# A two-layer decoder: one product buffer of the value stage takes the place of the first key weights

## The chip, the cores and the metric

The kernel runs on one core of a Trainium2 chip. The metric is the device time of one execution in microseconds, the median of several runs; less is better. An execution on the core has five instruction queues that run beside each other and wait for each other by semaphores: PE (matrix products), DVE (vector work), ACT (activations, here often copies out of the accumulator memory PSUM), POOL (a second, slower vector engine) and SP (which here only issues DMAs). Each queue works strictly in its own order.

## What is computed

Two transformer layers over a batch of 4 sequences of 256 tokens, 512 wide, in float32, with a layer norm after each of the four blocks:

```python
x = _layernorm(x + _L0_attn_ref(x, ...))   # attention with low-rank queries, keys and values, 32 heads
x = _layernorm(x + _L0_ffn_ref(x, ...))    # gated feed-forward, integer weights with scales
x = _layernorm(x + _L1_attn_ref(x, ...))   # causal attention, 32 heads
x = _layernorm(x + _L1_ffn_ref(x, ...))    # linear layer plus eight low-rank experts
```

The change touches the second attention only. Its projections are

```python
q = jnp.einsum('bsd,de->bse', hidden_states, wq).reshape(B, S, H, DQ)
kv = jnp.einsum('bsd,de->bse', hidden_states, wkv)
k = kv[..., :H * DN].reshape(B, S, H, DN)
v = kv[..., H * DN:H * (DN + DV)].reshape(B, S, H, DV)
```

where `H` is 32 and `DN` and `DV` are 128. The scores, the causal mask, the softmax, the product with `v` and the output projection follow.

## The kernel before

**Products with fewer multiplications.** Every large product is computed by a scheme of seven block products instead of eight, applied twice, one within the other (7 x 7 products in place of 8 x 8). Each of the seven "outer" products `i` (0 to 6) is itself made by seven "inner" ones. The price is additions: combinations of the input blocks, of the weight blocks (`combinations`, L133, four subtractions or additions at L136 to L139) and of the results.

**The value stage.** It lies between the first feed-forward block and the second attention (about 648 to 832 us of the profile). It makes the values of all 32 heads in four groups `g` of two times four heads (`NV`, `stages_v`). A group is seven units `p`, one for each outer product `i = OUTER[p // 2][p % 2]`, in the order 2, 0, 1, 4, 3, 6, 5. The list `vorder` (L669) puts 28 units in a row: the first two of group 3, the first two of group 2, then the rest of groups 3, 2, 1 and 0.

In a unit, `seven` (L787) issues seven inner products on PE (L969 in `multiply`), each 128 x 512 out, as four matmul records. They go to three PSUM banks; two units in turn use the banks `b0, b1, b2` and `s, t, o`. ACT (L800) and DVE (L803) empty the banks, with the additions of the inner scheme, into a buffer for the outer product `i`. At the end of the unit, `end` adds this buffer to the results by `add` (L952): four additions of 128 x 512, three on POOL and one on DVE, all at L956. `store` (L958, DMA at L962) writes finished values of groups 1 to 3 to DRAM, from where the attention reads them back. Group 0 stays in SBUF.

**The buffers of the outer products.** `block()` hands them out, four in turn: the two halves of `x` (x[0:4] and x[4:8], free here because `x` has been saved to DRAM at L746), then the slots s8 and s9, then s10 and s11. A slot holds 128 x 1024 numbers. The slots s0 to s7 hold results of odd groups. In the attention the twelve slots hold queries and keys.

**What else runs in the stage.** `input_blocks2` (L774), called once in the second unit, makes the combinations of the inputs: some on DVE (L772 and L531 to L534), and three sets (`blocks2(i, nc.gpsimd)`) on POOL. The combined value and query weights were prepared in the first attention and lie in DRAM (`vw`, `qd`); `Stored.get` loads them, three units ahead, by two DMAs on SP into `qb` and `qc` (L504; the query weights by L502), with three buffers each.

**The first key weights.** Key weights are not prepared before. `Weights.load` (L831, DMA at L839) loads 1 MB of one group of four heads into the tile `w`, `combine` makes the outer combinations on POOL (into `c`), and `get` the inner ones (`inner_left`, into `cc`, and partly in place in `w`). For group 0 these three are the first entries of the list `first`: `load`, `combine`, the `get` of the first key unit. The `get` of the first three query units are the entries 3 to 5. The function `begin`, which runs ahead of every value unit, calls them: entries 0, 1 and 2 ahead of the units 21, 22 and 23 of 28, and entries 3, 4 and 5 ahead of the units 25, 26 and 27.

**What sets the order.** The order in which this code issues the work is not the order on the queues: a scheduler orders each engine's instructions when the program is built, by its own estimate of when they can start. The place of a call in the code is a priority, not a position.

**Behind the value stage.** The queries and keys of group 0 follow (L874 in `stages_qk`): first four query units, then four key units. The first of each writes straight into slots; the others write into `parts`, which lie in `x`: the second unit in x[4:8], the third in x[0:4], the fourth in x[4:8] again. `add` at L895 sums them up, half on DVE and half on POOL for group 0. All these products use the banks b0, b1 and b2. The attention itself begins at about 876 us.

Of the kernel before, what the change touches and what calls it, by code (L numbers as in the profile page):

```python
# [9 lines left out]
F32 = mybir.dt.float32  # L10
# [6 lines left out]
P = 128  # L17
# [3 lines left out]
DC = D // P  # L21
NH = 32
GH = 4
NG = NH // GH
DN, DR, DV = 128, 64, 128
# [13 lines left out]
def tile_decoder2(ctx: ExitStack, tc: tile.TileContext, a: dict, out: bass.AP):  # L39
# [497 lines left out]
    with tc.tile_pool(name="f0", bufs=1) as f0:  # L537
# [131 lines left out]
        vorder = [(3, 0), (3, 1), (2, 0), (2, 1)]  # L669
        vorder += [(g, p) for g in (3, 2, 1, 0) for p in range(7) if (g, p) not in vorder]  # L670
        with tc.tile_pool(name="f0d", bufs=2) as f0d:
# [62 lines left out]
            for tt in range(NT // 2):  # L734
# [7 lines left out]
                for m in range(2):  # L742
                    t = 2 * tt + m
# [18 lines left out]
    with banks("ps1", b0=1, b1=1, b2=1, s=2, t=2, o=1), \  # L762
# [11 lines left out]
        def input_blocks2():  # L774

            for t in (NT - 2, NT - 1):
                turned(t, nc.scalar.copy)
            xcomb(3, xblock(1, 1), xblock(0, 1))
            xcomb(4, xblock(0, 1), xblock(0, 0))
            xcomb(1, xblock(1, 1), right[4])  # L780
            blocks2(1)
            blocks2(4)
            xcomb(5, xblock(1, 0), right[1])
            for i in (3, 6, 5):
                blocks2(i, nc.gpsimd)

        def seven(multiply, shape, dst, scale=1.0, tags=("b0", "b1", "b2"), hold="p1", bufs=2):  # L787

            st, o = {}, {}
            b0, b1, b2 = tags  # L790

            def product(i, tag, first):

                if first:
                    st[tag] = bank(tag, (P, *shape))
                multiply(i, st[tag], first)
                return st[tag]

            def copy(key, acc):
                nc.scalar.activation(o[key], acc, AF.Copy, scale=scale)  # L800

            def plus(key, acc, other):
                nc.vector.scalar_tensor_tensor(o[key], acc, scale, o[other], ALU.mult, ALU.add)  # L803

            def first():
                o[None] = l1.tile([P, *shape], F32, tag=hold, name="p1", bufs=bufs)
                o.update({(n, m): dst(n, m) for n in range(2) for m in range(2)})
                copy(None, product(0, b0, True))

            return [  # L810
                first,
                lambda: plus((0, 1), product(1, b1, True), None),
                lambda: plus((1, 1), product(4, b2, True), None),
                lambda: copy((0, 0), product(2, b0, False)),
                lambda: plus((1, 1), product(3, b1, False), (1, 1)),
                lambda: plus((0, 1), product(6, b2, False), (0, 1)),
                lambda: plus((1, 0), product(5, b1, False), None),
            ]
# [46 lines left out]
        def stages_qk(pr, g, store, scale):  # L865
# [3 lines left out]
            def units_of(p):  # L869
# [46 lines left out]

                us = seven(multiply, (len(pair), Q), dst, scale, tags_next())
                us[0] = lambda u=us[0]: (begin(), u())
                us[-1] = lambda u=us[-1]: (u(), end())
                return [(u, len(pair)) for u in us]  # L920
# [3 lines left out]
        def stages_v(g):  # L924

            pr, heads, st = pv[g], (2 * g, 2 * g + 1), {}

            def block(i=None):

                if i is None:  # L930
                    i = turnx[0] = (turnx[0] + 1) % 4
                    if i < 2:
                        return [x[:, 4 * i + 2 * k:4 * i + 2 * k + 2, :] for k in range(2)]
                    i += 2
                return [
                    l1.tile([P, 2, GH * DV], F32, tag=f"s{2 * i + k}", name="vb", bufs=1) for k in range(2)
                ]

            def result(n, m):

                if (n, m) not in st:
                    if g % 2:
                        st[n, m] = block(2 * n + m)
                    else:
                        h = heads[n]
                        if h not in v:
                            v[h] = l1.tile([P, NT, GH * DV], F32, tag="v", name=f"v{h}")
                        for mm in range(2):
                            st[n, mm] = [v[h][:, 4 * mm + 2 * k:4 * mm + 2 * k + 2, :] for k in range(2)]
                return st[n, m]  # L950

            def add(out, l, r):  # L952
                for k in range(2):
                    for t in range(2):
                        eng = nc.vector if k and t else nc.gpsimd
                        eng.tensor_tensor(out[k][:, t], l[k][:, t], r[k][:, t], ALU.add)  # L956

            def store(n, m):  # L958
                if g:
                    for k in range(2):  # L960
                        t0 = 4 * m + 2 * k
                        nc.sync.dma_start(out=vd[heads[n]][:, t0:t0 + 2, :], in_=st[n, m][k])  # L962

            def stage(p, tags):
                i = OUTER[p // 2][p % 2]

                def multiply(k, acc, first):
                    for t in range(2):
                        nc.tensor.matmul(  # L969
                            acc[:, t, :].rearrange("p (h c) -> p h c", h=2),  # L970
                            inner[i][k][:, t * P:(t + 1) * P], pr.inner[i][k],
                            start=first and t == 0, stop=True, skip_group_check=True,
                        )

                def dst(n, m):
                    if n == m == 0:
                        st[i] = result(0, 0) if i == 2 else result(0, 1) if i == 0 else block()
                    return st[i][m][:, :, n * 2 * DV:(n + 1) * 2 * DV]

                def end():  # L980
                    u = st.get(0)
                    if i == 0:
                        add(st[2], st[2], u)
                        store(0, 0)
                    elif i == 1:
                        add(u, u, st[1])
                    elif i == 4:
                        add(result(1, 1), u, st[4])
                    elif i == 3:
                        add(result(1, 0), u, st[3])  # L990
                    elif i == 6:
                        add(u, st[1, 1], st[6])
                        store(0, 1)
                        add(st[1, 1], st[1, 1], st[3])
                        store(1, 1)
                    elif i == 5:
                        add(st[1, 0], st[1, 0], st[5])
                        store(1, 0)

                us = seven(multiply, (2, 2 * DV), dst, tags=tags)  # L1000
                us[-1] = lambda u=us[-1]: (u(), end())
                return us

            return stage
# [139 lines left out]
        for g in range(NG):  # L1144
# [10 lines left out]
            else:  # L1155
                first = [wk.load, wk.combine, *(st["ahead"] for st in (sk[0], *sq[:3]))]
# [28 lines left out]
        for n, us in enumerate(vunits):  # L1185
            def begin(n=n, u=us[0]):
                if n + 3 < len(vorder):
                    later = vorder[n + 3]
                    pv[later[0]].get(later[1])
                else:  # L1190
                    first[n + 6 - len(vorder)]()
                if len(vorder) - 7 <= n < len(vorder) - 4:
                    first[n + 7 - len(vorder)]()
                u()
                if n == 1:
                    input_blocks2()

            us[0] = begin
# [3 lines left out]
        def units_of(stages):  # L1202

            units = []
            for st in stages:
                def begin(st=st):
                    for key in ("load", "att", "next"):
                        if key in st:
                            st[key]()

                (u, w), rest = st["units"][0], st["units"][1:]
                units += [((lambda begin=begin, u=u: (begin(), u())), w), *rest]
            return units
# [197 lines left out]
```

## Time and profile before

| | |
|---|---|
| median of 3 runs | 1683.13 us (1682.35 to 1692.36) |
| the profiled execution: time | 1681.63 us |
| the profiled execution: span of the core's work | 1679.6 us |
| mean granted PE clock | 0.997 of full speed |
| PE busy | 1644.5 us, 98% of the span |
| DVE busy | 1064.9 us, 63% |
| ACT busy | 700.8 us, 42% |
| POOL busy | 1104.5 us, 66% |
| chain that ended last | PE 88%, DVE 7%, POOL 2%, DMA 1%, ACT 1% |

All places below are microseconds from the start of the span. A line of a timeline gives the start, the duration, the engine, the source line, the operation, the output and inputs by the program's names, how many instructions were merged, and in brackets how long the engine stood idle before and what ended that. "SPq" is SP's queue, which issues DMAs. A duration of merged instructions covers all of them.

In the stages around the change PE's matmuls follow each other at one record in 0.216 us when nothing stops them. What counts in this profile is where PE does not keep that pace.

### The profile page before, as it was taken

Reading aid. Unit: us, or ns where it says so; the run is one execution under the profiler, and the core shown is the slowest. Engines: PE = TensorE matmul, PEld = TensorE weight load, DVE = VectorE, ACT = ScalarE, POOL = GpSimd, SP = SyncE. Lnnn points to the kernel's source line nnn. Section 1 sums busy time; section 2 is a strip of 40 time slices with the busy share of each in tenths; the row PEclk is TensorE's granted clock in tenths of the full one; section 3 lists DMA queues with packets and bytes.
Section 4 is the critical chain, followed back from the end, with each engine's and each line's share of the span. In section 5 each row is a group of like instructions: output and inputs, shape, how many; then the busy total and the mean of one; then the engine's idle time right before and its main releaser. Section 6 shows DMA issues by size and latency. Waiting matters only on the chain.

```text
span 1679.6 us, 24076 instructions
## 1 busy us (share of the span) xinstructions
PE 1644.5 (98%) x7954; PEld 1294.9 (77%) x7954; DVE 1064.9 (63%) x2345; ACT 700.8 (42%) x2070; POOL 1104.5 (66%) x1330
## 2 busy tenths in 40 slices
PE   8999999999999998999999999999999999999998
PEld 5566666666488887888878888888888878888854
DVE  3577777777745536677777666666666775433454
ACT  1566666667422202111125555555555553200043
POOL 1988888881437445786667767677676777689530
PEclk9999999999999999999999999999999999999999
DMA  9465555451312002687524334253342344443000
GB/s 345 152 211 215 217 199 205 175 194 50 108 43 77 13 26 73 200 262 248 187 76 128 115 98 144 71 178 118 95 140 73 122 176 161 155 151 125 26 18 33
DMA packets 96251, 226.88 MB, mean 135 GB/s; under 512 B 10272, under 2 KB 53792, under 8 KB 90112
## 3 DMA queue, kind: packets, MB, share of 16 engines
q1 hardware_dynamic: 94464, 224.54, 38.9%
q8 instruction: 63, 1.03, 0.3%
q10 hardware_dynamic: 1664, 0.81, 0.2%
q14 instruction: 60, 0.49, 0.1%
HBM read 140.38 MB, written 84.93 MB: 134 GB/s over the span
## 4 chain that ended last, share of the span: by engine, by line
PE 88%; DVE 7%; POOL 2%; DMA 1%; ACT 1%; issue 1%; DVEq 0%; SPq 0%; POOLq 0%; ACTq 0%
PE ps_b L874 19%; PE ps_s L63 13%; PE ps_b L1059 11%; PE ps_b L969 5%; PE ps_o L1135 4%; PE ps_o L396 3%; PE ps_s L612 3%; PE ps_t L379 3%; PE ps_p L294 3%; PE ps_t L1126 2%; PE ps_o L63 2%; PE ps_t L969 2%; PE ps_o L612 2%; PE ps_p L612 2%; PE ps_b L63 2%; PE ps_p L302 2%
## 5 line engine op out<-in xcount | busy, mean ns | idle before, releaser
L1108 ACT ACTIVATE pr<-ps_s,nmx 128x128 f32<-128x128 f32 (+1 forms) x256 | 105.0, 416 | 105.0 <-DVE nmx L1104 101.9
L355 ACT ACTIVATE pr<-ps_s,ebias 128x256 f32<-128x256 f32 x256 | 117.7, 472 | 48.5 <-DVE ebias L350 46.9
L1068 DVE TENSOR_TENSOR x<-ps_b,x 128x512 f32<-128x512 f32 x96 | 66.2, 690 | 105.0 <-PE ps_b L1059 97.5
L63 PE MATMUL ps_s<-kT,qh 128*128 128x256 f32 x512 | 129.1, 393 | 1.1 <-ACT pr L355 1.1
L1120 ACT ACTIVATE pr<-pr,rc 128x128 f32<-128x128 f32 (+1 forms) x256 | 103.8, 448 | 56.6 <-DVE rc L1118 55.0
L1100 DVE TENSOR_TENSOR ps_s<-ps_s,mask 128x256 f32<-128x256 f32 x128 | 55.2, 431 | 106.5 <-PE ps_s L63 106.5
L63 PEld LDWEIGHTS ps_s<-kT,qh 128*128 128x128 f32 x512 | 91.5, 189 | 37.6 <-issue 20.2
L803 DVE SCALAR_TENSOR_TENSOR x<-ps_b,p 128x512 f32<-128x512 f32 (+1 forms) x159 | 96.3, 607 | 22.9 <-PE ps_b L874 13.3
L344 DVE TENSOR_REDUCE nmx<-ps_s 128x2 f32<-128x512 f32 x128 | 84.9, 683 | 25.1 <-PE ps_s L63 24.2
L136 POOL TENSOR_TENSOR ws<-ws 128x128 f32<-128x128 f32 (+1 forms) x128 | 70.7, 567 | 45.6 <-DMA ws<-in_wq 27.4
L370 DVE TENSOR_SCALAR pr<-pr,rc 128x256 f32<-128x256 f32 x192 | 93.9, 515 | 4.4
L1078 POOL TENSOR_TENSOR x<-x,po 128x512 f32<-128x512 f32 x48 | 60.1, 1267 | 37.0 <-DVE x L1068 28.7
L1135 PE MATMUL ps_o<-pT,v 128*128 128x256 f32 x256 | 82.4, 404 | 0.6 <-DVE pT L1128 0.6
L1104 DVE TENSOR_REDUCE nmx<-ps_s 128x1 f32<-128x128 f32 (+1 forms) x256 | 79.4, 351 | 3.8
L1128 DVE COPY pT<-ps_t 128x384 f32<-128x384 f32 x128 | 70.3, 549 | 10.7 <-PE ps_t L1126 10.3
L800 ACT ACTIVATE p<-ps_b 128x512 f32<-128x512 f32 (+1 forms) x78 | 43.1, 552 | 75.3 <-PE ps_b L874 43.8
L396 PEld LDWEIGHTS ps_o<-pT,cN 128*64 128x64 f32 x512 | 31.8, 136 | 54.8 <-issue 22.3
L803 DVE SCALAR_TENSOR_TENSOR x<-ps_b,x 128x512 f32<-128x512 f32 (+1 forms) x106 | 64.2, 606 | 15.3 <-PE ps_b L874 8.7
L396 PE MATMUL ps_o<-pT,cN 128*64 128x256 f32 x512 | 69.4, 391 | 3.0 <-DVE pT L383 2.6
L139 POOL TENSOR_TENSOR ws<-ws,ws 128x128 f32<-128x128 f32 (+1 forms) x128 | 70.4, 564 | 2.4
L138 POOL TENSOR_TENSOR ws<-ws 128x128 f32<-128x128 f32 (+1 forms) x128 | 70.8, 567 | 1.3
L137 POOL TENSOR_TENSOR ws<-ws 128x128 f32<-128x128 f32 (+1 forms) x128 | 70.1, 563 | 1.3
(692 smaller groups left out, 4616.7 us busy)
## 6 DMA issues: line engine op xcount, KB each, us to landing
attd<-att SPq DMA_DIRECT2D x128, 128.0 KB, 1.8
vw<-ws SPq DMA_DIRECT2D x56, 256.0 KB, 2.4
qd<-ws SPq DMA_DIRECT2D x56, 256.0 KB, 2.3
qb<-vw SPq DMA_DIRECT2D x28, 512.0 KB, 4.4
qb<-qd SPq DMA_DIRECT2D x24, 512.0 KB, 4.4
v<-vd SPq DMA_DIRECT2D x6, 2048.0 KB, 8.0
qc<-vw SPq DMA_DIRECT2D x28, 384.0 KB, 3.9
vw<-ws SPq DMA_DIRECT2D x24, 384.0 KB, 2.5
```

The source lines that it names most:

```text
L63: nc.tensor.matmul(o, l, r, start=(i == 0), stop=(i == len(pairs) - 1))
L355: nc.scalar.activation(pr[:, i, qt, :], sc[:, qt, :], AF.Exp, bias=bias[:, i, qt:qt + 1], accum_out=sm[:, i, qt:qt + 1],)
L370: nc.vector.tensor_scalar(prs, prs, rc[:, i, qt:qt + 1], None, ALU.mult)
L396: nc.tensor.matmul(po[i * RKV:(i + 1) * RKV, :], cN[:, 2 * b + kt, :], pTs[i][:, kt, :], start=(kt == 0), stop=(kt == 1),)
L612: nc.tensor.matmul(banks_of[tag], lhs[i][:, k, :], rhs[i][:, k, :], start=first and k == 0, stop=k == 1, skip_group_check=True,)
L803: nc.vector.scalar_tensor_tensor(o[key], acc, scale, o[other], ALU.mult, ALU.add)
L874: nc.tensor.matmul(acc[:, e, :], pr.inner[i][k], inner[i][k], start=first and e == 0, stop=True, skip_group_check=True,)
L969: nc.tensor.matmul(acc[:, t, :].rearrange("p (h c) -> p h c", h=2), inner[i][k][:, t * P:(t + 1) * P], pr.inner[i][k], start=first and t = ...
L1059: nc.tensor.matmul(st[tag][:, tt, :], box["left"][i][:, k, (t0 + tt) * P:(t0 + tt + 1) * P], box["right"][i][:, k, :], start=first and tt ...
L1108: nc.scalar.activation(pr[:, pt, :], sc[:, pt, :], AF.Exp, bias=nmx[:, qt:qt + 1], accum_out=sm[:, qt:qt + 1],)
L1120: nc.scalar.activation(pr[:, pt, :], pr[:, pt, :], AF.Copy, scale=rc[:, qt:qt + 1])
L1135: nc.tensor.matmul(po, v[g][:, 2 * b, hv], pT[:, 0:2, :], start=True, stop=False)
```

## The change

The third of the four product buffers of `block()` is now the tile `w` in place of the slots s8 and s9; the fourth is s8 and s9 in place of s10 and s11. The slots s10 and s11 are no longer used in the value stage. Because `w` exists once (`bufs=1`), the first key weights can be loaded only when the value stage has used this buffer for the last time; the three entries of `first` that load and combine them are called ahead of the units 25, 26 and 27 in place of 21, 22 and 23.

```diff
                     i = turnx[0] = (turnx[0] + 1) % 4
                     if i < 2:
                         return [x[:, 4 * i + 2 * k:4 * i + 2 * k + 2, :] for k in range(2)]
-                    i += 2
+                    if i == 2:
+
+                        t = l1.tile([P, DC, GH * DV], F32, tag="w", name="vb", bufs=1)
+                        return [t[:, 2 * k:2 * k + 2] for k in range(2)]
+                    i += 1
                 return [
                     l1.tile([P, 2, GH * DV], F32, tag=f"s{2 * i + k}", name="vb", bufs=1) for k in range(2)
                 ]
...
                     pv[later[0]].get(later[1])
                 else:
                     first[n + 6 - len(vorder)]()
-                if len(vorder) - 7 <= n < len(vorder) - 4:
-                    first[n + 7 - len(vorder)]()
+                    first[n + 3 - len(vorder)]()
                 u()
```

Nothing else is changed: the same arithmetic, the same instructions and the same DMAs.

## The prediction

> **What bounds the kernel now.** I read the page first. PE is busy 98% of the span and holds 88% of the chain that ended last, so a microsecond counts only if PE stands still for it, or runs at a lower clock. The value stage's products, `ps_b L969` and `ps_t L969`, hold 5% and 2% of it: the change can act only there and just behind. So I cut the stage (648 to 840 us) into windows. A row has busy time and instructions by engine, then granted clock, DMA share, GB/s.
>
> ```profile
> core 0: us, PE busy (x) PEld busy (x) DVE busy (x) ACT busy (x) POOL busy (x), PEclk, DMA share, GB/s
> 645.00:660.00 15.00, 13.36 (x70) 11.66 (x69) 6.79 (x16) 6.47 (x14) 6.13 (x7) 1.00 0.40 132
> 660.00:680.00 20.00, 16.40 (x67) 13.47 (x66) 18.43 (x26) 2.76 (x5) 19.77 (x27) 0.91 0.32 91
> 680.00:700.00 20.00, 17.88 (x76) 15.11 (x75) 11.26 (x16) 3.21 (x6) 13.62 (x10) 0.91 0.69 243
> 700.00:720.00 20.00, 19.93 (x93) 17.23 (x92) 15.64 (x21) 3.58 (x6) 16.31 (x13) 1.00 0.62 192
> ```
>
> From 700 on PE does 92 to 95 matmul records in 20 us, to the stage's end. In 660 to 700 it does 67 and 76: at 0.216 us a record, 5.6 and 3.7 us are lost. Only there has PE something to win. POOL's timeline (start, duration) shows why POOL is late there:
>
> ```profile
> 653.87 1.27 POOL L136 TENSOR_TENSOR c<-w 128x512 f32<-128x512 f32 x1 [16.17 <-DMA w<-in_wk]
> ...
> 660.03 1.86 POOL L137 TENSOR_TENSOR w<-w 128x128 f32<-128x128 f32 x2
> ...
> 679.93 4.17 POOL L956 TENSOR_TENSOR vb<-vb 128x512 f32<-128x512 f32 x3
> 684.06 3.71 POOL L956 TENSOR_TENSOR v<-v 128x512 f32<-128x512 f32 x3
> ```
>
> The key weights are combined first, 653.87 to 669.82; then POOL makes its input blocks (L531 to L534, to 679.93) and only then the first value adds. SP's queue, where a store stands in front of a load, and PE, which waits for that load:
>
> ```profile
> 677.04 0.32 SPq L504 DMA_DIRECT2D qc<-vw  x1
> 684.13 0.32 SPq L962 DMA_DIRECT2D vd<-vb  x1
> 684.54 0.38 SPq L504 DMA_DIRECT2D qb<-vw  x1
> ```
>
> ```profile
> 689.48 1.83 PE L969 MATMUL ps_s<-qb,xT 128*128 128x256 f32 x4 [2.12 <-DMA qb<-vw]
> 691.10 1.91 PE L969 MATMUL ps_b<-qb,x 128*128 128x256 f32 x4
> 692.81 1.22 PE L969 MATMUL ps_t<-qc,x 128*128 128x256 f32 x4
> ```
>
> The store waits for POOL's add (679.93 + 4.17 = 684.10), the load lands 4.9 us after its issue, PE stands 2.12 us. Then the twelve records up to 693.86 take 4.38 us, not 2.59: the clock costs 1.79 more. At the other end of the stage, POOL, DVE, PE:
>
> ```profile
> 814.18 4.32 POOL L956 TENSOR_TENSOR v<-v,vb 128x512 f32<-128x512 f32 x3 [1.71 <-issue]
> ...
> 834.98 3.74 POOL L956 TENSOR_TENSOR v<-v,x 128x512 f32<-128x512 f32 x3
> ```
>
> ```profile
> 840.92 1.46 DVE L803 SCALAR_TENSOR_TENSOR x<-ps_b,p 128x512 f32<-128x512 f32 x2 [0.79 <-PE ps_b L874]
> ```
>
> ```profile
> 842.35 1.03 PE L874 MATMUL ps_b<-x,qc 128*128 128x256 f32 x4
> ```
>
> POOL's last value adds end at 838.72. They read x[4:8]; the second query stage overwrites x[4:8] from 840.92 on, with 2.2 us to spare. PE's product at 842.35 needs the bank that this DVE instruction empties. So POOL has no more than about 3 us of slack here.
>
> **The change part by part.** Comparing the two programs' instruction lists, engine by engine, PE, DVE and ACT keep their order to the last row. Only 20 POOL instructions (4 of 512 columns, 16 of 128) and one DMA move.
>
> *Removed at the start.* SP's load of w at 648.68 waited 14.5 us; what it was in front of (two stores at 650.33, a load at 656.52) waits for its own data until then, so going earlier is worth nothing to them. On POOL 15.95 us go (653.87 to 669.82). POOL's first block needs the copy that ended at 658.95; eight blocks' instructions at 0.69 us fit before DVE's last combination (L772, 669.47, done 670.9), the last four end at about 674. The first value adds then wait for DVE (vb written by 675.9): 680.1 instead of 684.10. The store leaves at 680.1, the load behind it at about 680.4, since PE frees its buffer at about 679; it lands by 685.3, before 687.2, when PE asks for it. Gain: 2.12 + 1.79 = 3.9 us. If another load were late next, it would be the stage's next qb, issued at 685.85: its buffer is free from 683 and it is wanted at 693.
>
> The rest of the loss stays: from 658.99 to 671.47 DVE works without a gap, and PE's 2.52 us at 671.60 end on it. Whether DVE gets faster or slower depends on what POOL does beside it. The row: DVE's 128x256 subtractions start every 0.33 us at 633 to 635 with POOL quiet and every 0.60 at 665 to 669 beside POOL's 128x128, so a POOL instruction of 0.41 us holds DVE for 0.27. Scaled to the 128x256 blocks (0.55 of 0.69), and interleaving them one by one, L772 starts at 669.5 instead of 669.47: nothing won or lost. The Trainium skill, "SBUF — State Buffer", section "Who interferes with whom", speaks against the change: a DVE instruction with two SBUF inputs and a GpSimd one that reads SBUF exclude each other, and the holder keeps the port for the whole instruction. With 0.69 instead of 0.55 L772 starts at 670.5, so the gain would be 2.9. I take the row, which is of this pair of engines and line. The other bound is DVE undisturbed: PE's stalls of 1.08 and 2.52 and their clock go too, about 5 us more. No row supports that, since POOL stays busy beside DVE.
>
> For the clock the skill has a rule as well ("TensorE: Matmul & The Clock Gate", "HAM oscillation — how this bites in real kernels"): gaps over about 3.4 us are to be avoided. By it 2.12 us of idleness costs no clock, and the gain is 2.1 only. The rows above show the slow records after a 2.12 us gap, so I take 3.9.
>
> *Buffers.* Of the four product buffers used in turn, the third lies in w, the fourth in what was the third. A buffer still comes round every fourth time: no wait added, cost nothing. The last use of w as a product buffer is read by the adds at 814.18.
>
> *Added at the end.* The load of w waits for those adds (818.50) behind the last vw load on SP (815.07), and lands 5.0 to 5.2 us later by the two loads of its kind (648.68 to 653.87, 880.26 to 885.27): 823.7. Other end: shared with the two query loads behind it (0.9 MB) at the 200 GB/s of that window, 9 us. I take 5.2, as the queue has it first. The query loads (819.39, 821.12) come up to 5 us later and are needed at 832.66: covered.
>
> On POOL the first of the 20 instructions of the combination stands behind the first add of the next three (820.16), ends that wait at 823.7, and the other two adds are interleaved with it. Then 4 x 1.23 + 16 x 0.41 = 11.5 us, which is what the same 20 take at 885 to 898 (12.78, less a foreign one of 1.23). For 128x128 there are two rows, 0.41 here and 0.93 at 660.03 above, beside DVE's 1024-column instructions; DVE's work at the end reads PSUM and only one SBUF tensor, as at 861 to 865, where it is 0.41 to 0.47, so I take 0.41, and 1.5 us for four DVE additions in between. With the two adds (2.5) POOL is at 823.7 + 11.5 + 2.5 + 1.5 = 839.2 (before: 826.27). Then nine adds of 1.25: 850.4 instead of 838.72.
>
> DVE's write at 840.92 waits for the last of them, and with it the whole in-order DVE queue (all evacuations of ps_b); ACT's write to the same x at 842.61 waits too. PE's 842.35 goes at 850.4 + 0.75 = 851.15: 8.8 us of standstill. The clock costs 1.8 more by the rows at 689.48. POOL's own query adds (840.21) run after 850.4, in step with the shifted PE. Loss 10.6 us. The combined weights are ready at 839 and wanted at 853.60: no wait there.
>
> Sum: -3.9 + 10.6 = +6.7 us against the profiled execution (span 1679.6, time 1681.63). The median of the runs is 1683.13, 1.5 above it; carried over, 1689.8.
>
> **The rivals.** *A faster kernel, the last adds not gating PE.* If DVE's write at 840.92 waits for an older reader of x[4:8] (the adds at 808.14), POOL may be 11.7 us late without a trace in PE: -3.9 us, 1679.2. It decides if POOL's end must be later than 851 to stop anyone. Against it: in the changed program that write still lists POOL among its waits, and these adds are the last readers before it. Chance 0.09; with DVE undisturbed too it reaches 1674, still not 1% faster.
>
> *Slower by over 1%, the port shared at the worst rate.* If at the end POOL pays what its worst rows show (16 at 0.93: +8.3; thirteen of 512 columns at 1.62, as at 852.67, not 1.25: +4.8), it ends at 863.5, PE loses 23.7, the sum is +19.8: 1702.9. It passes +16.8, 1%, when POOL ends 10.1 us later than I reckon, at 860.5. For it: four two-input additions of DVE fall into the stretch before 841. Against it: once DVE is stopped at 841, POOL has the port alone. Chance 0.17, with whatever else I don't see that lengthens a standstill.
>
> *Nothing moves,* because the load is hoisted again: excluded by the instruction lists.
>
> **How the numbers follow.** Likeliest (0.74): 1689.8, and between 1685 (load and adds at their best, DVE a little faster) and 1696 (load at 9 us, start gain 2). The range for 8 in 10 takes that and the lower part of the slower rival: 1683 to 1700. One per cent, 16.8 us, is about what a measurement of this kernel can tell from no change. Both the likeliest case and the faster rival lie within it: 0.79; slower over 1%: 0.17; faster over 1%: 0.04, for what I don't see, since all that PE loses from 660 to 700 is 9.3 us.
>
> **What would show it.** In the changed profile: SP's load of w near 818, not 648; L531 on POOL at 659; no wait of PE on qb near 687; 660 to 680 still with about 67 records, 680 to 700 with over 85; L136 to L139 on POOL between 824 and 839; an idle DVE from 841 ended by POOL, and a PE gap of 8 to 9 us in the second query stage with a lower granted clock after it. I am wrong if that gap is under 3 us or over 18, or if PE's early loss doesn't shrink.

## The result, and the profile after

| | before | after |
|---|---|---|
| median of 20 runs | 1682.41 us (1677.92 to 1692.38) | 1688.10 us (1684.61 to 1701.84) |
| ratio, 95% interval | | 1.0033 [1.0020, 1.0047] |
| the profiled execution: time, span | 1681.63, 1679.6 us | 1684.61, 1682.5 us |

The changed kernel is slower by 5.7 us. Its profiled execution is the fastest of its twenty, which matters below. It also came to the stage 1.58 us earlier than that of before did (the first value product starts at 649.46, not 651.04), so absolute places are shifted by that much, and lengths are counted from that product.

| us | before | after |
|---|---|---|
| from the first value product to the second `ps_b<-qc,t` product (start of the stage) | 51.46 | 45.45 |
| from the first value product to the first query product (value stage) | 181.62 | 176.36 |
| query units, up to the first key product | 20.94 | 31.48 |
| key units up to the first score product | 22.19 | 22.18 |
| sum of the last three | 224.75 | 230.02 |

The difference is +5.3 us in this pair of profiles, and it has two parts: the value stage wins 5.3, the query units lose 10.5. First the start, in the windows of after (busy time and instructions by engine, then clock, DMA share, GB/s):

```profile
core 0: us, PE busy (x) PEld busy (x) DVE busy (x) ACT busy (x) POOL busy (x), PEclk, DMA share, GB/s
660.00:680.00 20.00, 16.66 (x76) 13.93 (x75) 19.32 (x28) 3.58 (x6) 15.21 (x15) 1.00 0.39 114
680.00:700.00 20.00, 20.00 (x94) 17.61 (x93) 13.97 (x21) 3.58 (x6) 14.56 (x12) 1.00 0.78 262
820.00:840.00 20.00, 14.85 (x66) 11.91 (x64) 10.67 (x15) 2.39 (x4) 19.92 (x26) 0.97 0.35 101
840.00:860.00 20.00, 16.47 (x59) 12.83 (x60) 12.04 (x19) 3.16 (x6) 10.12 (x9) 0.77 0.31 92
```

From 680 on PE is full (94 records, 76 before), and both early windows are at clock 1.00 where before had 0.91. The lost records have moved to 820 to 860: 66 and 59, at 0.97 and 0.77, where before had 92 and 84 at 1.00. The queues of after say why. POOL, then SP, then PE:

```profile
657.51 1.70 POOL L531 TENSOR_TENSOR x<-xT 128x256 f32<-128x256 f32 x1 [21.40 <-ACT xT L128]
...
672.04 4.18 POOL L960 TENSOR_TENSOR vb<-vb 128x512 f32<-128x512 f32 x3
678.61 1.78 POOL L960 TENSOR_TENSOR v<-v 128x512 f32<-128x512 f32 x1 [2.39 <-DVE v L803]
```

```profile
676.25 0.32 SPq L966 DMA_DIRECT2D vd<-vb  x1
676.66 0.38 SPq L504 DMA_DIRECT2D qb<-vw  x1
```

```profile
669.75 1.13 PE L973 MATMUL ps_o<-qc,xT 128*128 128x256 f32 x4 [3.29 <-DVE vb L803]
670.72 0.59 PE L973 MATMUL ps_b<-qc,x 128*128 128x256 f32 x2
671.15 1.03 PE L973 MATMUL ps_t<-qb,x 128*128 128x256 f32 x4
```

POOL starts its input blocks when the copy has ended, not after a combination; its first adds run from 672.04, the store leaves at 676.25, the load behind it at 676.66, and PE has no wait on `qb` any more. One wait is left at the start, 3.29 us for DVE, and the products behind it run at full speed (1.03 us for four). Behind its wait at this place, before was slower (1.91 us for four):

```profile
671.60 1.13 PE L969 MATMUL ps_o<-qc,xT 128*128 128x256 f32 x4 [2.52 <-DVE vb L803]
...
673.27 1.91 PE L969 MATMUL ps_t<-qb,x 128*128 128x256 f32 x4
```

At the end of the stage, SP, POOL, DVE and PE of after:

```profile
810.87 0.33 SPq L839 DMA_DIRECT2D w<-in_wk  x1
```

```profile
815.73 1.27 POOL L136 TENSOR_TENSOR c<-w 128x512 f32<-128x512 f32 x1 [1.39 <-DMA w<-in_wk]
...
830.66 0.46 POOL L139 TENSOR_TENSOR cc<-w,cc 128x128 f32<-128x128 f32 x1
...
838.88 3.69 POOL L960 TENSOR_TENSOR v<-v,x 128x512 f32<-128x512 f32 x3
```

```profile
832.82 0.68 DVE L803 SCALAR_TENSOR_TENSOR slot_(True, 1)_6969<-ps_b,p 128x512 f32<-128x512 f32 x1
842.60 1.29 DVE L803 SCALAR_TENSOR_TENSOR x<-ps_b,p 128x512 f32<-128x512 f32 x2 [9.10 <-POOL v L960]
```

```profile
843.35 2.08 PE L874 MATMUL ps_b<-x,qc 128*128 128x256 f32 x4 [7.68 <-DVE x L803]
```

The load lands 4.9 us after its issue, POOL combines and then makes its last adds, to 842.57. DVE's write into x[4:8] waits 9.10 us for exactly that, PE waits 7.68 us for DVE, and its next four products take 2.08 us, not 1.03: the clock is down.

### The profile page after: what moved, and what is told of

Read it like the earlier page. It is cut to its first block, busy times and chain, and to the rows that moved or that the text cites. A ratio compares the mean times of both kernels' runs of the same rounds, so it can differ in the third digit from the quotient of the medians.

```text
span 1682.5 us, 24074 instructions
## 1 busy us (share of the span) xinstructions
PE 1642.7 (98%) x7954; PEld 1294.0 (77%) x7954; DVE 1064.5 (63%) x2345; ACT 701.3 (42%) x2070; POOL 1104.9 (66%) x1330
## 3 DMA queue, kind: packets, MB, share of 16 engines
q8 instruction: 63, 1.03, 0.3%
## 4 chain that ended last, share of the span: by engine, by line
PE 87%; DVE 7%; POOL 3%; ACT 1%; DMA 1%; issue 1%; SPq 0%; DVEq 0%; POOLq 0%; ACTq 0%
PE ps_b L874 19%; PE ps_s L63 13%; PE ps_b L1063 11%; PE ps_b L973 4%; PE ps_o L1139 4%; PE ps_o L396 3%; PE ps_s L612 3%; PE ps_t L379 3%; PE ps_p L294 3%; PE ps_t L1130 2%; PE ps_o L63 2%; PE ps_o L612 2%; PE ps_p L612 2%; PE ps_b L63 2%; PE ps_t L973 2%; PE ps_p L302 2%
```

## The experiments

Two theories. Mine: the key weights' combination, put behind the value stage by the shared buffer, makes POOL's last adds late, and these hold x[4:8], so DVE and PE stand; at the start POOL's early adds free SP's queue. The rivals: the calls' place does it; the gap at the end comes from the load itself or has other gates; the early wait on `qb` is a matter of bandwidth. Times are medians; ratios are to before on the same chip.

**e1_late_calls.** The calls moved, the buffers as before.

```diff
-                if len(vorder) - 7 <= n < len(vorder) - 4:
-                    first[n + 7 - len(vorder)]()
+                    first[n + 3 - len(vorder)]()
```

> Only the second hunk of the change: the calls of load and combine move to the units 25 to 27, the product buffers stay as before. The instruction lists come out the same as before on every engine. Theory (the buffer, not the place of the call, moves the combination): the kernel of before, ratio 1.000 within its noise, load of w at the end of the feed-forward block, PE's stalls of about 2.5 and 2.1 us at the start of the value stage. Rival (the late call is what counts): about +5.5 us as in the changed kernel. It is also a second look at the clock behind the 2.5 us stall: if the low clock there depends on the phase of a window and not on the length of the stall, it may be missing this time.

1682.38 us, ratio 1.0007 [0.9997, 1.0016]. The instruction lists of all engines were those of before, so this is before once more: the later calls alone move nothing. The work moves only when the buffer is shared; the shared buffer without the later calls was not run. As a second profile of that program it has one surprise. PE's timeline has its waits at the start at the same places (the one on the load is longer, since PE comes to it sooner), and after neither do the products run at the low clock:

```profile
675.11 1.13 PE L969 MATMUL ps_o<-qc,xT 128*128 128x256 f32 x4 [2.52 <-DVE vb L803]
...
676.51 1.03 PE L969 MATMUL ps_t<-qb,x 128*128 128x256 f32 x4
...
692.87 1.13 PE L969 MATMUL ps_s<-qb,xT 128*128 128x256 f32 x4 [3.69 <-DMA qb<-vw]
693.84 1.03 PE L969 MATMUL ps_b<-qb,x 128*128 128x256 f32 x4
```

Here the start takes 49.84 us, not 51.46.

**e2_parts_apart.** The changed kernel, but the second query unit of group 0 writes its parts into s10 and s11, which the change had left free. (The cut leaves out the lines that read the parts from there.)

```diff
...
+                    elif g == 0 and p == 1 and store is qn:
+                        parts[p] = [
+                            l1.tile([P, 2, GH * DV], F32, tag=f"s{10 + k}", name="part", bufs=1) for k in range(2)
+                        ]
                     else:
                         parts[p] = x[:, 4 * (p % 2):4 * (p % 2) + 4, :]
```

> The changed kernel, but the second query unit of group 0 writes its parts into the slots s10 and s11, which are free there, not into x[4:8]. POOL's work and order stay as they are. Theory (PE's gap at the end is DVE's write to x[4:8] waiting for POOL's last value adds): the gap of 7.7 us and the low clock behind it go, under 1.5 us of loss is left there, and the start gain of 6.0 stays: about 5 us faster than before, ratio 0.997, 10 to 11 us faster than the changed kernel. Rival (a late POOL stops PE anyway, by its query adds or by the combined weights coming late): the gap turns up again within 15 us, ratio 1.002 or more.

1679.20 us, 0.9988 [0.9977, 1.0000]: the gain was smaller than I had expected, but the mechanism is clear. DVE and POOL of this run:

```profile
842.20 1.48 DVE L803 SCALAR_TENSOR_TENSOR part<-ps_b,p 128x512 f32<-128x512 f32 x2 [0.55 <-PE ps_b L874]
```

```profile
847.06 4.64 POOL L971 TENSOR_TENSOR v<-v,x 128x512 f32<-128x512 f32 x3
```

POOL's last adds end at 851.7, as late as ever (this profile's stage begins 5.3 us later than that of after), and yet DVE writes its parts at 842.20 and waits for PE alone. The query units take 21.24 us, against 31.48 in after and 20.94 in before. So behind the value stage POOL's lateness cost time only through the space x[4:8]; within it, a wait of 0.80 us for DVE at 831.10 stays.

**e6_before_parts.** The same edit in before, as a control.

> Before, with the products of the second query unit of the first group in two free slots instead of x[4:8], the one part that was added to after in e2_parts_apart. My theory: in before POOL's last adds are done when TensorE gets there, so the space gates nothing; ratio 1.000 (0.9985 to 1.001), and the 0.9988 of e2_parts_apart is the gain of the early adds alone. Rival: the query stage of before gains from the slots itself (fewer waits on x behind 838), ratio 0.9985 or lower, and e2 shows nothing of the change.

1681.58 us, 0.9995 [0.9985, 1.0005], query units 20.99 us: in before the space gates nothing. The intervals of the two ratios overlap, so the times do not prove that e2 keeps a gain from the early adds. Nor does the way to the first score product: 223.08 us in e2, 224.58 here, but 223.12 in e1, which is before's program. What e2's profile does show is less waiting at the start, 3.29 us on DVE against 1.06 and 2.51 on DVE and 3.61 on the load here.

**e5_dose.** The changed kernel with one POOL subtraction done five times over.

```diff
-            def combine(self):
+            def combine(self, more=False):
                 self.left = left(self.whole, thirds(cmb.tile([P, 3, 2, 2 * DN], F32, tag="c", name="c")))
+                if more:
+                    for _ in range(4):
+                        nc.gpsimd.tensor_tensor(self.left[1], self.left[4], self.left[0], ALU.subtract)
...
-                first = [wk.load, wk.combine, *(st["ahead"] for st in (sk[0], *sq[:3]))]
+                first = [wk.load, lambda wk=wk: wk.combine(True), *(st["ahead"] for st in (sk[0], *sq[:3]))]
```

> After, with the 512-column subtraction that makes s2 of the first key weights done five times over instead of once (the same values each time): 4 x 1.23 = 4.9 us more on POOL near 817, nothing else changed. My theory, that POOL's work in front of the last value adds passes one for one into TensorE's wait for the space of x[4:8]: the wait of 7.68 us in front of the bias product near 843 becomes 12.6 us, and the kernel 1.003 x after, 1.006 of before (1.0045 to 1.0075). Rival, that the gap comes from the late landing of the weights or from a full queue and POOL has slack: the wait stays near 7.7 us, 1.003 of before.

1693.02 us (6 runs), 1.0062 [1.0038, 1.0087]. PE of this run:

```profile
852.37 2.08 PE L877 MATMUL ps_b<-x,qc 128*128 128x256 f32 x4 [13.54 <-DVE x L803]
```

The query units take 36.51 us, 5.03 more than in after, for 4.9 us of POOL. The wait itself is 13.54 and not 12.6, because a wait of 0.82 us that after had at 822.94 is part of it now. POOL's work passes into PE's gap one for one.

**e3_mid_stage.** `w` serves as a buffer for the first two groups only, then s10 and s11; load and combination come in mid-stage.

```diff
-                    if i == 2:
+                    if i == 2 and g > 1:
...
-                    i += 1
+                    i += 1 if i == 3 else 3
...
-                    first[n + 3 - len(vorder)]()
+                if 14 <= n < 14 + 3:
+                    first[n - 14]()
```

> w is a product buffer for the value groups 3 and 2 only, for groups 1 and 0 it is s10 and s11 as before; load and combination are called at the units 14 to 16, and stand on POOL before the first adds of group 1. Theory (the place on POOL decides, and in the middle POOL has about 6 us free ahead of that and 1.8 in each unit): the start gains the same 6.0 us, the end is as before, the middle costs 0 to 3 us since the value adds come late but buffers come round only every fourth unit: ratio 0.9965 to 0.998. Rival (11.5 us on POOL cost PE about as much wherever the value adds need POOL): a PE gap near 750 to 790, ratio 1.000 or more.

1685.17 us, 1.0020 [1.0012, 1.0029]: my theory's number failed, the rival's gap came. POOL, SP and PE of this run:

```profile
755.96 1.27 POOL L136 TENSOR_TENSOR c<-w 128x512 f32<-128x512 f32 x1 [6.48 <-DMA w<-in_wk]
```

```profile
772.16 0.32 SPq L966 DMA_DIRECT2D vd<-vb  x1
```

```profile
779.04 2.08 PE L973 MATMUL ps_s<-qb,xT 128*128 128x256 f32 x4 [6.29 <-DMA qb<-vw]
```

POOL stands 6.48 us for the weights, combines to 769.7, its value adds are late, and so is the store that waits for them at 772.16; the loads behind it in SP's queue are late too, and PE stands 6.29 us. This is the wait that the change takes away at the start, come back in the middle. Two things make POOL late here, the wait for the weights and the combination, and this run does not part them; what it shows is that there is no room for both at this place.

**e9_before_store and e4_load_other_queue.** Is that really the queue? In e9 the eight stores of the first value group are issued by POOL, in e4 the one held-up load by ACT; both are otherwise before.

```diff
-                        nc.sync.dma_start(out=vd[heads[n]][:, t0:t0 + 2, :], in_=st[n, m][k])
+                        (nc.gpsimd if g == vorder[0][0] else nc.sync).dma_start(
+                            out=vd[heads[n]][:, t0:t0 + 2, :], in_=st[n, m][k])
```

```diff
-                    nc.sync.dma_start(out=t, in_=src[:, p])
+                    (nc.scalar if self is pv[3] and p == 3 and tag == "qb" else nc.sync).dma_start(out=t, in_=src[:, p])
```

> Before, with the eight stores of the first value group (those near 684) issued from POOL, whose adds they wait for, and not from SP; so no load of weights stands behind a store in SP's queue. My theory, that before's wait on qb is a load held up in SP's queue by a store that waits for POOL's late adds: TensorE's wait of 2.1 us (3.6 to 3.7 in two other profiles of the same start) near 690 goes, POOL pays some tenths of a us for each issue; ratio 0.9985 of before (0.997 to 1.000). Rival: the load is late by its bandwidth or by its buffer, the wait stays, 1.000 to 1.001.

> The kernel before, with one DMA moved: the load of qb for the sixth value unit is issued on ACT's queue, where no store stands in front of it. POOL is untouched. Theory (PE's 2.1 us at 689.5 is this load behind the store that waits for POOL): the stall goes, and the slow clock behind it: -2 to -4 us, ratio 0.998. Rival (the start gain of the changed kernel comes from DVE or POOL being faster at the start): the load comes early, but PE stands at the same place for another reason, ratio 1.000.

e9 1681.20 us, 0.9993 [0.9982, 1.0004]; e4 1681.46 us, 0.9998 [0.9984, 1.0012]. In both the wait on that `qb` is gone, so it was the queue. But the times show no gain clear of noise, and PE finds another wait some instructions on. e9, then e4:

```profile
694.27 1.13 PE L970 MATMUL ps_t<-qc,x 128*128 128x256 f32 x4 [2.01 <-DVE vb L803]
```

```profile
697.21 1.10 PE L969 MATMUL ps_b<-qb,t 128*128 128x256 f32 x4 [0.74 <-DMA qb<-vw]
```

In e9 POOL is as late as in before (its first adds begin 28.7 us after the first value product, 28.9 there), and for a part of the time that PE no longer waits for a load it waits for DVE. One addition of DVE, among POOL's additions, takes 4.31 us there; in before its like took 0.69 (688.13):

```profile
688.71 4.31 DVE L956 TENSOR_TENSOR vb<-vb 128x512 f32<-128x512 f32 x1
```

It comes back at 715.49 with 3.75 us, and PE waits 1.46 us at 720.50. e4 has neither: its waits at the start are 1.14, 2.52 and 0.74 us, against 1.08, 2.52 and 2.12 in before and 1.29, 2.52 and 3.69 in e1, and it comes to the first score product in 221.70 us (224.75 and 223.12). Its interval reaches down to 2.7 us under before, so its time neither shows nor excludes a gain of 1.4 us or more.

**e8_after_again.** The changed kernel unaltered, for a second profile.

> The changed kernel once more, unaltered, for its profile. If the granted clock behind a stall is a matter of chance, the wait of 3.29 us near 670 may now be followed by products at the low clock (pairs of products of 2.08 us in place of 1.03[...]), as in e2_parts_apart; if it is fixed by the program, the products behind it run at full clock again. The waits themselves, 3.29 and 7.68 us, should stand within 0.1 us in either case.

1687.21 us. The waits repeat, the clock does not. PE of this run, to be set beside after's 1.13, 0.59 and 1.03 shown above:

```profile
670.71 2.07 PE L973 MATMUL ps_o<-qc,xT 128*128 128x256 f32 x4 [3.29 <-DVE vb L803]
...
847.23 2.07 PE L874 MATMUL ps_b<-x,qc 128*128 128x256 f32 x4 [7.70 <-DVE x L803]
```

The start takes 48.19 us here and 45.45 in after: 2.74 us of clock behind one and the same wait, paid in one execution and not in the other. To the first score product the two differ by 1.7 us, since the clock behind the second wait took less here; their spans differ by 2.9 us (1685.4 and 1682.5).

**e7_parts_blocks, e10_parts_store, e11_all.** Towards a kernel better than both. e7 is e2 with block 4 of the inputs on POOL, to shorten DVE's chain before PE's 3.29 us wait; e10 is e2 with e9's edit; e11 has all three.

```diff
-            blocks2(4)
+            blocks2(4, nc.gpsimd)
```

> e2_parts_apart, and block 4 of the input combinations (four subtractions of 128x256) issued on POOL instead of VectorE: VectorE's chain in front of the evacuation of the first ps_o is 4 instructions, some 3.4 us, shorter, and POOL has 4 x 0.73 to 0.9 = 2.9 to 3.6 us more before its first value adds. My theory: TensorE's wait of 3.29 us on that evacuation falls under 0.5 us, with the clock that sometimes follows it; ratio 0.9965 of before (0.995 to 0.998). Rival: POOL becomes late with block 4 and TensorE waits for it instead, or the first store slips behind its 676 again and the wait on qb of some 2 us comes back: 0.9985 to 1.001.

> e2_parts_apart with those eight stores issued from POOL too. There the first value adds are early, and no wait on qb is left at the start; theory: nothing more is won, 0.9988 of before (0.9975 to 1.000), and no wait over 1 us between 672 and 700. Rival: issuing from POOL costs over 1 us each and puts POOL late, ratio over 1.000.

> e7_parts_blocks with those eight stores issued from POOL: what is left there at the start is a wait of 1.47 us on VectorE and one of 2.68 us on a load of qb that SP issued behind a store at 678. Theory: the second goes, ratio 0.997 of before (0.9955 to 0.9985), the fastest kernel of the study. Rival: that load then waits for its buffer and not for the queue, or POOL's issues delay its adds: 0.9985 to 1.000.

| | us | ratio to before | start of the stage | to first score |
|---|---|---|---|---|
| e7_parts_blocks | 1680.58 | 0.9988 [0.9971, 1.0005] | 46.77 | 221.45 |
| e10_parts_store | 1683.65 | 1.0006 [0.9998, 1.0014] | 45.45 | 221.95 |
| e11_all | 1680.24 | 0.9991 [0.9984, 0.9997] | 44.29 | 220.93 |

In e7 both expectations came half true: the wait on DVE shrinks to 1.47 us, and the wait on a load behind a store is back. PE of e7, then of e11:

```profile
668.26 1.13 PE L984 MATMUL ps_t<-qb,x 128*128 128x256 f32 x4 [1.47 <-DVE vb L803]
685.23 1.13 PE L984 MATMUL ps_s<-qb,xT 128*128 128x256 f32 x4 [2.68 <-DMA qb<-vw]
```

```profile
672.78 1.13 PE L985 MATMUL ps_t<-qb,x 128*128 128x256 f32 x4 [1.47 <-DVE vb L803]
```

In e11 the second wait is gone as expected, and its stage is the shortest of all, 3.8 us under before's profile; by its time it beats before by 0.09%, less than the 0.3% that I had expected. e10 missed: its stage is 2.8 us shorter than that of before, its time is not. Its profile shows a lower clock at 540 to 560 and at 1360 to 1400, far from the edit, but so does that of e2, whose median is 1679.20; why e10 misses is open. Stores on POOL also have a price: in e10 and e11, as in e9, one addition of DVE takes 3.76 or 3.77 us, and PE waits 1.45 or 1.47 us for it, at 720.49 and 717.81. Of the three, e11 alone is faster than before by an interval that excludes 1, and barely; among ten measured ratios that is weak evidence.

## Why the prediction was right, step by step

The forecast was 1689.8 us with the change slower by 6.7; measured are 1688.1 and 5.7. Of the 1.7 us between forecast and time, 0.7 is the base: I carried the sum over to a median of 3 runs, 1683.13, which over 20 runs is 1682.41. That the rest is only 1.0 us is partly luck. The two profiles of after's program and the two of before's (e1 is the second) make four pairs, and in these the way to the first score product grows by 5.3 to 8.6 us, depending on the clock behind the waits.

- *Start, POOL and SP.* Shown. First adds done at 676.2 (with the 1.58 us of shift 677.8; forecast 680.1), the load right behind the store, no wait on `qb`, over 85 records in 680 to 700 (94). The blocks ended as forecast (672.04, or 673.6 with the shift; 674), though the first three of the eight that I had at 0.69 us each took 1.70 to 1.77: POOL had to wait for DVE's last combination anyway, to 669.17, and that took it up. The adds, though, did not then wait for DVE until 675.9, as I had reckoned: they follow without a gap.
- *DVE's chain, "nothing won or lost".* Right in the sum: from the start of the first L772 to the instruction that empties `ps_o` 11.88 us before, 11.62 after. The stretch up to the 128x256 instructions became 1.1 us shorter (5.71 to 4.61), the eight of these 1.1 us longer (4.77 to 5.87). Beside POOL's 128x256 subtractions DVE starts its own every 0.87 us, against 0.34 when POOL is quiet, so a POOL instruction of 0.69 holds DVE for 0.53, where I had scaled to 0.55. The Trainium skill ("SBUF — State Buffer", "Who interferes with whom") calls the port that the two share an exclusive lock; held for the whole 0.69, it would by my forecast have cost another 1.0 us, and this stretch of the trace does not show that. DVE's timeline in after shows both cadences; POOL is busy to 667.0 and then idle to 669.17:

```profile
665.49 0.94 DVE L532 TENSOR_TENSOR x<-xT,x 128x256 f32<-128x256 f32 x1
666.35 0.94 DVE L534 TENSOR_TENSOR x<-t,x 128x256 f32<-128x256 f32 x1
667.21 0.41 DVE L533 TENSOR_TENSOR x<-xT 128x256 f32<-128x256 f32 x1
667.55 0.41 DVE L534 TENSOR_TENSOR x<-xT,x 128x256 f32<-128x256 f32 x1
```

- *Start gain, 3.9 us.* This is the mis-sized term. In the profiled pair it is 6.0 (51.46 to 45.45), since the clock behind the remaining wait, which I had left standing, was not charged in after; by after's second profile it is 3.3, and from e1's profile to that one 1.7. The late load had also hidden the clock: in before PE went on behind it 38.44 us after the first value product, in e1, where no clock had been lost, after 38.51. With that wait gone, PE came to the same product after 34.22 us in after and after 36.97 in its second profile, so taking the wait away was worth 1.5 to 4.2 us of before's time, not 2.12. The step that failed is "The rows above show the slow records after a 2.12 us gap, so I take 3.9": it makes the clock a fixed price of the gap. "About 67 records" in 660 to 680 fell with it: 76 in after, 63 in its second profile. The skill's rule ("TensorE: Matmul & The Clock Gate", "HAM oscillation — how this bites in real kernels"), that gaps over about 3.4 us are to be avoided, does no better if it is read as saying that shorter ones cost no clock: 2.52 us were followed by the low clock in before and in e4, and not in e1 and e9.
- *Load of w.* Issue 810.87, that is 818.5 less shift and gain; landing 4.9 us later (5.2 forecast).
- *Combination and POOL's end.* From the landing to the end of the last adds 26.8 us (815.73 to 842.57), forecast 26.7 (823.7 to 850.4).
- *PE's gap, 8.8 us and 1.8 of clock.* The query units are 10.5 us longer: 7.68 of wait and 2.9 of clock; with 0.75 us around the wait at 822.94, where DVE is late beside POOL, which I had not foreseen, the end costs 11.3 instead of 10.6. The second profile has 7.70 and 1.6, so here too only the clock varies.
- *Rivals.* The faster one (the last adds gate nobody) is out: e2 takes the gate away and the gap goes, e5 lengthens the work and the gap grows by the same. The slower one needed POOL at its worst rates; the 128x128 instructions stayed at 0.46, but for one pair of 1.33.

Net: -6.0 + 11.3 = +5.3 in the profiled pair, +7.0 between before and the second profile of after (with e1 as before, +6.9 and +8.6).

## What to carry to other kernels

A buffer borrowed from data that an idle engine prepares early moves that preparation to the end of the loan. Ask what stands behind it in that engine's queue there, and whose space that work still reads: here 12.4 us of POOL (815.73 to 831.07, less two additions, 2.9 together) became 7.7 us of TensorE, and two spare slots for the next writer gave them back. Where one queue carries stores that wait for results and loads that are wanted soon, a late engine shows up as a late load; moving the load or the store to another queue removed the wait that was seen, and smaller ones came up behind it (0.74 us with the load on ACT's queue, 2.01 and 1.46 with the stores on POOL's).

## What the runs showed of the hardware that was not expected

The clock behind a wait of TensorE is not a property of the wait. The same program, at the same instruction, with the same 3.29 us, went on at full clock in one execution (after) and lost 2.7 us in another (e8). Whether these two ran on one chip is not on record, but e2 and e3 did: there too one wait of 3.29 us was followed by the low clock and the other was not. In the profiles around the changed stage, seven of fifteen waits of 2.12 to 3.69 us were followed by the low clock; the four of 6 us and more (6.29, 7.68, 7.70 and 13.54) all were. That whole executions differ for the same reason fits the 159 timed runs of before in the experiments: the medians were 1683.3, 1682.2, 1680.9 and 1680.3 us at a mean granted clock of 0.996, 0.997, 0.998 and 0.999 (26, 67, 52 and 8 runs), and the six runs at 0.993 to 0.995 took 1689 to 1693 us. What decides when the clock is lowered was not tried. A single profile thus can't price a wait of this length to better than some 3 us, half of what this change is worth.

The second surprise is DVE's addition of 128x512. Around the changed stage it took at most 1.81 us in the ten profiles of kernels whose stores SP issues. In each of the three kernels in which POOL issues the stores of the first value group (e9, e10, e11), one or two took 3.75 to 4.31 us, among POOL's additions and stores. That they come with the stores on POOL is seen in all three; the mechanism was not tried.
